# Storing token rows and their norm factors together, after the first score rows, in a fused attention and expert kernel

## The chip, the cores and the metric

The kernel runs on one core of a Trainium2 chip. The metric is device time in microseconds of one execution; lower is better. The engines are TensorE (PE, matrix products and transposes), VectorE (DVE), ScalarE (ACT), GpSimd (POOL) and SyncE (SP, which only issues DMAs here). Each takes its instructions in program order. The core's DMAs run on sixteen DMA engines. A DMA with run-time row numbers (a gather or a scatter) is issued by POOL.

## The reference

`x` is 8 x 256 tokens of 256 values in float32, 2048 tokens in all. Four blocks follow, each added to `x`:

```python
x = x + L0_xattn(layernorm(x), ctx, ctx)    # correlation attention
x = x + L0_ffn(layernorm(x))                # eight experts, balanced
x = x + L1_xattn(layernorm(x), ctx)         # 16-head softmax attention
x = x + L1_ffn(layernorm(x))                # shared and top-2 experts
```

The change lies in the second block. Its experts pick tokens one after another: each takes the 256 tokens with the highest score among those that no earlier expert took.

```python
def balanced_assignment(scores):
    for e in range(E):                       # E = 8, C = 256
        s = jnp.where(taken, -jnp.inf, scores[:, e])
        _, idx = jax.lax.top_k(s, C)
        parts.append(idx)
        taken = taken.at[idx].set(True)
...
routed = feat[sort_by_expert].reshape(E, C, D)
h = layer_norm(routed, ln_g, ln_b)
h = gelu(einsum("ecd,edf->ecf", h, w1) + b1)
h = einsum("ecf,efd->ecd", h, w2) + b2
out = routed + h                             # rows go back to their tokens
```

## The kernel before

`fast_path` writes out the order of all work by hand; the program order of each engine is the order of the lines. It has these stages: the correlation attention (to about 44 us); the rows that come out of it, with their norms and the expert scores (44 to 55); seven searches for the experts' thresholds, with the expert products beside them (55 to about 222); the softmax attention; the last experts.

**Rows and factors.** `X` holds the tokens in SBUF, 128 partitions by 16 tiles of 256 values. `copy_rows` puts the rows of a batch into PSUM with a product by the identity, `spread_rows` adds the attention's output, and `take` (line 2006 issues its store) or `act_sums` (line 2023) copies the sum back to `X`, takes its statistics, and stores the rows of that batch on SP into `NMd`, a DRAM table of 2048 rows of 258 floats. The last two floats of a row are its norm's scale and shift (`rm`); `store_factors` (line 1944) writes these with four DMAs of 512 pieces of 8 bytes.

**Scores.** `SC` holds the scores, and SP stores it to DRAM (`SCd`, line 2178). `load_row(e)` (line 2170) reads expert e's row of it back, spread over all partitions: four groups of tokens, 32 copies of each. After the score store SP issues, in this order: rows 1 and 2, the four factor stores, rows 3 to 6, a 2 MB store of zeros to `Yd` (the experts' output table, line 2183), and one of zeros to the spare rows of `Od` (line 2187).

**Searches.** `search(e)` finds expert e's threshold in five rounds. In each round DVE counts the scores above 32 trial levels (`above`, line 2203), PE sums the counts over partitions (`pcn`, line 2220), and DVE picks the next level (`few`, line 2225, `t`, line 2230). `list_tokens(e)` then turns the choice into 256 row numbers (`pid` on PE, `ids` on DVE) and lets POOL gather those rows and their factors from `NMd` into `R` (line 2341), with two DMAs of 128 rows.

**The work beside them.** `work` is a queue of small PE pieces. `fill(us)` takes pieces from its front until their planned cost has used up `us`:

```python
while work and us > 0.3:
    cost, do = work.popleft()
    do()
    us -= cost
```

The queue starts with 32 steps of `keys` and 20 of `vals` (planned at 0.43 each, one product of 256 columns per step, two steps to a tile). The second step of a tile ends with an ACT copy (`KT` or `VA`) that frees its PSUM slot in `ps_k`, which has two. `search` calls `fill(head)` before its first round's sum, `fill(each[r - 1] - 0.86)` before each later one, and `fill(0.86)` after each of the first four. `FILLS` gives `head` and `each`. Steps of `steps_of(e)` run after each of these rounds.

`ffn(e, ...)`, called by `start_ffn`, normalises the two gathered tiles on ACT (line 2383), puts `turn_rows` (four transposes and two ACT operations that give `RT`) at place 3 of `work`, and appends 16 `up` steps (`ph`) and 16 `down` steps (`py`), then the load of expert e+2's weights (`load_l0`). Before the change the first expert's `ffn` is called after search 1 ends; expert e's, for later ones, in the third round of search e+2.

Of the kernel before, what the change touches and what calls it, by code (L numbers as in the profile page):

```python
# [9 lines left out]
F32 = mybir.dt.float32  # L10
# [9 lines left out]
P = 128  # L20
# [1066 lines left out]
def fast_path(  # L1087
# [33 lines left out]
    nc = tc.nc  # L1121
# [26 lines left out]
    res = ctx.enter_context(tc.tile_pool(name="res", bufs=1))  # L1148
    small = ctx.enter_context(tc.tile_pool(name="small", bufs=3))
    dram = ctx.enter_context(tc.tile_pool(name="dram", bufs=1, space=DRAM))  # L1150
    X = res.tile([P, NT, D], F32, name="X")
    hn = ctx.enter_context(tc.tile_pool(name="hn", bufs=2))
    nfine = res.tile([P, 1], F32, name="nfine")
    bad0 = res.tile([P, 1], F32, name="bad0")
# [684 lines left out]
    def copy_rows(b, pool, tag):  # L1839
        pos[b] = pool.tile([P, TPB, D], F32, tag=tag, name="po")  # L1840
        nc.tensor.matmul(  # L1841
            pos[b].rearrange("p h d -> p (h d)"),
            ident,
            rows_of(b).rearrange("p h d -> p (h d)"),
            start=True,
            stop=False,
            skip_group_check=True,
        )
# [90 lines left out]
    rowv = NMd.rearrange("(c p) d -> p c d", p=P)  # L1939
    sexp = pa.tile([P, NT, 32], F32, name="sexp")  # L1940

    def store_factors(m):
        for h in range(TPB):
            nc.sync.dma_start(
                out=NMd.rearrange("(g m h p) d -> m h p g d", m=2, h=TPB, p=P)[m, h][
                    :, :, D:
                ],
                in_=rm[:, 8 * m : 8 * m + 8, :].rearrange(
                    "p (g h) d -> h p g d", h=TPB
                )[h],  # L1950
            )


    psrs = []
# [41 lines left out]
    def take(bs, raw=False):  # L1996

        for b in bs:
            for h in range(TPB):
                q = TPB * order_b.index(b) + h  # L2000
                if raw:
                    nc.vector.bn_stats(st6[:, q, :], pos[b][:, h, :])
                else:
                    tile_stats(MV[:, q, :], pos[b][:, h, :])
            nc.scalar.copy(rows_of(b), pos[b])
            nc.sync.dma_start(
                out=rowv[:, TPB * b : TPB * (b + 1), 0:D], in_=rows_of(b)
            )

    sums = pa.tile([P, NT, 2], F32, name="sums")  # L2010
    sq = pa.tile([P, D], F32, name="sq")
# [1 line left out]
    def act_sums(b):  # L2013

        for h in range(TPB):
            q = TPB * order_b.index(b) + h
            nc.scalar.activation(
                rows_of(b)[:, h, :],
                pos[b][:, h, :],
                AF.Identity,  # L2020
                accum_out=sums[:, q, 0:1],
            )
        nc.sync.dma_start(out=rowv[:, TPB * b : TPB * (b + 1), 0:D], in_=rows_of(b))
        qs = slice(TPB * order_b.index(b), TPB * order_b.index(b) + TPB)
        nmean = small.tile([P, TPB], F32, tag="nmean", name="nmean")
        nc.gpsimd.tensor_scalar(nmean, sums[:, qs, 0], -1.0 / D, None, ALU.mult)
        nc.gpsimd.tensor_scalar(MV[:, qs, 0], sums[:, qs, 0], 1.0 / D, None, ALU.mult)

        def squares():
            for h in range(TPB):  # L2030
                q = TPB * order_b.index(b) + h
                nc.scalar.activation(
                    sq,
                    rows_of(b)[:, h, :],
                    AF.Square,
                    bias=nmean[:, h : h + 1],
                    accum_out=sums[:, q, 1:2],
                )
            nc.gpsimd.tensor_scalar(
                MV[:, qs, 1], sums[:, qs, 1], 1.0 / D, None, ALU.mult  # L2040
            )

        return squares
# [84 lines left out]
    raw_means()  # L2128
    means_a()
    means_2()  # L2130
    means_3(nc.gpsimd)

# [42 lines left out]

    nc.sync.dma_start(out=SCd, in_=SC)
    rows = {e: load_row(e) for e in range(1, 3)}
    for m in range(2):  # L2180
        store_factors(m)
    rows.update({e: load_row(e) for e in range(3, E - 1)})
    nc.sync.dma_start(
        out=Yd.rearrange("(c p) d -> p c d", p=P),
        in_=blank[:, 0:D].unsqueeze(1).to_broadcast([P, NT, D]),
    )
    nc.sync.dma_start(out=Od[T:, :], in_=blank[:, 0:D])

    def search(e, row, steps, head, each):

# [185 lines left out]
    def ffn(e, ids, R):  # L2376

        w1, w2, b2b = W0.pop(e)
        RT = pf.tile([P, KC, CAP], F32, tag="RT", name="RT")
        A = pf.tile([P, NF, CAP], F32, tag="A", name="A")  # L2380
        Y = pf.tile([P, NCT, D], F32, tag="Y", name="Y")
        for r in range(NCT):
            nc.scalar.activation(
                R[:, r, 0:D],
                R[:, r, 0:D],
                AF.Identity,
                bias=R[:, r, D + 1 :],
                scale=R[:, r, D : D + 1],
            )
            if e in TPART and r == NCT - 1:  # L2390

                nc.scalar.copy(blank[:, D : D + 1], blank[:, D + 1 : D + 2])
                n0_, n1_ = TPART[e]
                nc.sync.dma_start(
                    out=Td.rearrange("(n p) w -> p n w", p=P)[:, n0_:n1_, :],
                    in_=blank.unsqueeze(1).to_broadcast([P, n1_ - n0_, ROW]),
                )

        def turn_rows():
            prt = ps_t.tile([P, KC, NCT, P], F32, tag="pt", name="prt")  # L2400
            for r in range(NCT):
                for kc in range(KC):
                    nc.tensor.transpose(
                        prt[:, kc, r, :], R[:, r, kc * P : (kc + 1) * P], ident
                    )
            for kc in range(KC):
                nc.scalar.activation(  # L2407
                    RT[:, kc, :],
                    prt[:, kc].rearrange("p r q -> p (r q)"),
                    AF.Identity,  # L2410
                    bias=gbc[:, 1, kc : kc + 1],
                    scale=gbc[:, 0, kc : kc + 1],
                )

        work.insert(min(3, len(work)), (0.5, turn_rows))

        def up(f):
            ph = ps_h.tile([P, CAP], F32, tag="ph", name="ph")
            for kc in range(KC):
                nc.tensor.matmul(  # L2420
                    ph,
                    w1[:, kc, f * P : (f + 1) * P],
                    RT[:, kc, :],
                    start=(kc == 0),
                    stop=(kc == KC - 1),
                )
                if kc < KC - 1:
                    yield
            nc.scalar.activation(  # L2429
                A[:, f, :], ph, AF.Gelu_apprx_tanh, bias=b1c[:, e, f : f + 1]  # L2430
            )
            yield

        def down(r):
            py = ps_k.tile([P, D], F32, tag="pm", name="py")
            for f in range(NF):
                nc.tensor.matmul(  # L2437
                    py,
                    A[:, f, r * P : (r + 1) * P],
                    w2[:, f, :],  # L2440
                    start=(f == 0),
                    stop=(f == NF - 1),
                )
                if f < NF - 1:
                    yield
            if e < 3:
                nc.scalar.copy(Y[:, r, :], py)
                nc.gpsimd.tensor_tensor(Y[:, r, :], Y[:, r, :], b2b, ALU.add)
            else:
                nc.vector.tensor_tensor(Y[:, r, :], py, b2b, ALU.add)  # L2450
            nc.gpsimd.indirect_dma_start(
                out=Yd,
                out_offset=bass.IndirectOffsetOnAxis(ap=ids[:, r : r + 1], axis=0),
                in_=Y[:, r, :],
                in_offset=None,
            )
            yield

        if e == E - 1:
            work.append((0.0, lambda: first_rows(False)))  # L2460
        for f in range(NF):
            in_steps(up(f), KC)
        if e == E - 1:
            final.append(Y)
            work.append((0.0, lambda: first_rows(True)))
        for r in range(NCT):
            in_steps(down(r), NF)
        if e + 2 < E:
            work.append((0.0, lambda: W0.update({e + 2: load_l0(e + 2)})))
# [17 lines left out]
    def steps_of(e):  # L2487

        for r in range(ROUNDS - 1):
            if e >= 2:  # L2490
                next(listers[e - 1], None)
            if 2 <= e < 6:
                move_x(4 * (e - 2) + r)
            if r == 2 and e >= 2:
                start_ffn()
            yield

    FILLS = {0: (1.29, [1.29] * 4), 1: (2.15, [1.29] * 4)}
    FILLS[2] = FILLS[3] = (2.15, [1.73, 2.58, 1.73, 1.73])
    for e in range(E - 1):  # L2500
        if e == 5:
# [14 lines left out]
        if e == 0:  # L2516
            for k, _ in enumerate(listers[0]):
                fill((0.86, 0.43, 1.29, 0.43)[k])
        elif e == 1:
            start_ffn()  # L2520
    last = [listers[E - 2], list_tokens(E - 1, hand_over)]
    for k in range(5):
        for lister in last:
# [982 lines left out]
```

## Time and profile before

| what | us |
|---|---|
| median of 6 runs | 883.55 (881.74 to 885.25) |
| the profiled execution, its own time | 884.3 |
| its span, first to last instruction | 882.6 |
| PE busy | 860.2 (97%) |
| DVE / ACT / POOL busy | 307.9 / 268.3 / 219.1 |
| mean granted TensorE clock | 0.992 |

Times inside the execution are counted from the first instruction. A busy PE means that it had a product under way; at a granted clock of 0.50 the same product takes twice as long. In a timeline a row gives start, duration, engine, line, operation, output and inputs, and in brackets the engine's idle time just before it and what is named as ending it. Where an instruction waited for several things, the one that came last by the profile is named, and if that had long been done, it was another. SP's rows are the issuing of DMAs, not the transfers.

### The profile page before, as it was taken

Reading aid. Unit: us, or ns where it says so; the run is one execution under the profiler, and the core shown is the slowest. Engines: PE = TensorE matmul, PEld = TensorE weight load, DVE = VectorE, ACT = ScalarE, POOL = GpSimd, SP = SyncE. Lnnn points to the kernel's source line nnn. Section 1 sums busy time; section 2 is a strip of 40 time slices with the busy share of each in tenths; the row PEclk is TensorE's granted clock in tenths of the full one; section 3 lists DMA queues with packets and bytes.
Section 4 is the critical chain, followed back from the end, with each engine's and each line's share of the span. In section 5 each row is a group of like instructions: output and inputs, shape, how many; then the busy total and the mean of one; then the engine's idle time right before and its main releaser. Section 6 shows DMA issues by size and latency. Waiting matters only on the chain.

```text
span 882.6 us, 11174 instructions
## 1 busy us (share of the span) xinstructions
PE 860.2 (97%) x4192; PEld 535.7 (61%) x4192; DVE 307.9 (35%) x1008; ACT 268.3 (30%) x500; POOL 219.1 (25%) x305
## 2 busy tenths in 40 slices
PE   8998899999999999999999999999999999999997
PEld 6655687778555555545658474746464656474746
DVE  7475777430646765552111212111111111111011
ACT  4353454242577766331010111121111111111110
POOL 7161232321326464323310020111111122111200
PEclk9998899999999999999999999999999999999999
DMA  8475357950330001271110636565646433311130
GB/s 248 161 221 171 130 151 223 320 192 30 113 98 25 2 14 38 52 290 49 68 56 25 191 110 178 155 179 153 181 149 174 159 93 109 89 13 12 15 105 28
DMA packets 87126, 105.22 MB, mean 119 GB/s; under 512 B 8824, under 2 KB 77656, under 8 KB 87032
## 3 DMA queue, kind: packets, MB, share of 16 engines
q1 hardware_dynamic: 78520, 91.10, 32.4%
q0 software_dynamic: 7920, 13.02, 6.9%
q8 instruction: 35, 0.57, 0.3%
q10 hardware_dynamic: 624, 0.30, 0.1%
q14 instruction: 27, 0.22, 0.1%
HBM read 80.60 MB, written 25.37 MB: 120 GB/s over the span
## 4 chain that ended last, share of the span: by engine, by line
PE 90%; DMA 4%; DVE 3%; POOL 2%; ACT 1%; issue 1%; SPq 0%; DVEq 0%; POOLq 0%
PE pgt L3126 19%; PE py L3148 19%; PE pu L3126 19%; PE py L2437 6%; PE ph L2420 6%; PE p L2703 4%; PE pv L2718 3%; DMA R<-NMd,ids 2%; PE pp L2769 2%; PE pp L2670 2%; PE pp L1392 1%; PE pp L1413 1%; PE po L1841 1%; PE pgu L3321 1%; DMA C<-in_ctx_dram 1%; PE pt L3182 1%
## 5 line engine op out<-in xcount | busy, mean ns | idle before, releaser
L3135 DVE TENSOR_TENSOR A<-A,pu 128x512 f32<-128x512 f32 x96 | 66.1, 688 | 365.1 <-PE pu L3126 358.4
L3134 ACT ACTIVATE A<-pgt 128x512 f32<-128x512 f32 x96 | 57.4, 598 | 271.4 <-PE pgt L3126 271.4
L3195 POOL DMA_INDIRECT Od<-Y,ids x32 | 49.5, 1548 | 305.2 <-ACT Y L3208 208.6
L3126 PE MATMUL pgt<-RT,wa 128*128 128x512 f32 x256 | 121.1, 595 | 0.0
L3126 PE MATMUL pu<-RT,wb 128*128 128x512 f32 x256 | 120.3, 592 | 0.0
L3148 PE MATMUL py<-wc,A 128*128 128x256 f32 x512 | 111.8, 379 | 0.0
L3148 PEld LDWEIGHTS py<-wc,A 128*128 128x128 f32 x512 | 96.7, 190 | 13.3 <-issue 0.5
L3126 PEld LDWEIGHTS pu<-RT,wb 128*128 128x128 f32 x256 | 48.6, 190 | 61.2 <-issue 60.0
L2711 ACT ACTIVATE ex<-p,scale 128x512 f32<-128x512 f32 x128 | 77.3, 690 | 27.5 <-PE p L2703 26.3
L3126 PEld LDWEIGHTS pgt<-RT,wa 128*128 128x128 f32 x256 | 47.6, 190 | 54.9 <-issue 54.5
L2420 PE MATMUL ph<-RT,w 128*128 128x256 f32 x256 | 66.7, 411 | 1.8 <-ACT RT L2407 1.6
L2437 PE MATMUL py<-w,A 128*128 128x256 f32 x256 | 61.9, 389 | 0.0
L2420 PEld LDWEIGHTS ph<-RT,w 128*128 128x128 f32 x256 | 48.1, 202 | 11.5 <-ACT RT L2407 2.3
L2437 PEld LDWEIGHTS py<-w,A 128*128 128x128 f32 x256 | 46.5, 190 | 6.5
L2943 POOL DMA_INDIRECT Td<-HP,to x32 | 31.6, 986 | 63.3 <-DMA Td<-HP,to 62.6
L2429 ACT ACTIVATE A<-ph,b1c 128x256 f32<-128x256 f32 x64 | 30.1, 473 | 55.3 <-PE ph L2420 52.2
L3126 PE MATMUL pgt<-HT,wa_-1_2749 128*128 128x512 f32 x96 | 45.5, 596 | 0.0
L3126 PE MATMUL pu<-HT,wb_-1_2750 128*128 128x512 f32 x96 | 45.1, 592 | 0.0
L3208 ACT ACTIVATE Y<-py,R 128x256 f32<-128x256 f32 x32 | 15.2, 474 | 96.5 <-PE py L3148 96.5
L2703 PE MATMUL p<-QM,KT 32*128 32x512 f32 x256 | 43.5, 640 | 0.4 <-DVE QM L2684 0.4
L3148 PE MATMUL py<-wc_-1_2751,A 128*128 128x256 f32 x192 | 41.9, 379 | 0.0
L3148 PEld LDWEIGHTS py<-wc_-1_2751,A 128*128 128x128 f32 x192 | 36.4, 190 | 5.8 <-issue 1.0
(463 smaller groups left out, 991.9 us busy)
## 6 DMA issues: line engine op xcount, KB each, us to landing
w<-in_L_ffn_w_dram SPq DMA_DIRECT2D x16, 1024.0 KB
wa<-in_L_ffn_w_e_dram SPq DMA_DIRECT2D x8, 1024.0 KB
wb<-in_L_ffn_w_e_dram SPq DMA_DIRECT2D x8, 1024.0 KB
wc<-in_L_ffn_w_e_dram SPq DMA_DIRECT2D x8, 1024.0 KB
R<-Td SPq DMA_DIRECT2D x8, 530.0 KB
sa<-in_L_ffn_w_e_dram SPq DMA_DIRECT2D x16, 256.0 KB
sb<-in_L_ffn_w_e_dram SPq DMA_DIRECT2D x16, 256.0 KB
sc<-in_L_ffn_w_e_dram SPq DMA_DIRECT2D x16, 256.0 KB
```

The costliest lines, as they stand in the source:

```text
L2420: nc.tensor.matmul(ph, w1[:, kc, f * P : (f + 1) * P], RT[:, kc, :], start=(kc == 0), stop=(kc == KC - 1),)
L2429: nc.scalar.activation(A[:, f, :], ph, AF.Gelu_apprx_tanh, bias=b1c[:, e, f : f + 1])
L2437: nc.tensor.matmul(py, A[:, f, r * P : (r + 1) * P], w2[:, f, :], start=(f == 0), stop=(f == NF - 1),)
L2703: nc.tensor.matmul(ps[g].rearrange("p m q -> p (m q)"), KT[rows, c, k0 : k0 + P], QM[b][rows, c].rearrange("p m q -> p (m q)"), start=True ...
L2711: nc.scalar.activation(e4[:, g], ps[g], AF.Exp, scale=scale)
L2718: nc.tensor.matmul(pvs[b, c][32 * g : 32 * g + 32, m, :], VA[:, b * TPB + kt, 8 * c + 2 * g + m, :], ex[b, c, kt][:, g, m, :], start=(kt = ...
L2943: nc.gpsimd.indirect_dma_start(out=Td, out_offset=bass.IndirectOffsetOnAxis(ap=to[g][:, k, j : j + 1], axis=0), in_=HP[:, GT * g + j, :], ...
L3126: nc.tensor.matmul(ps, w_[:, kc, fs], xs[kc], start=(kc == 0), stop=(kc == KC - 1),)
L3134: nc.scalar.activation(a, pgt, AF.Silu)
L3135: nc.vector.tensor_tensor(a, a, pu, ALU.mult)
L3148: nc.tensor.matmul(py, A[:, f, s : s + P], wc[:, f, :], start=(f == 0), stop=(f == NF - 1))
L3195: nc.gpsimd.indirect_dma_start(out=Od, out_offset=bass.IndirectOffsetOnAxis(ap=ids, axis=0), in_=Y, in_offset=None, compute_op=ALU.add,)
```

## The change

Six edits in `fast_path`:

1. `X` becomes a view of a wider tile `XF` with 258 floats per row, so that a row and its two factors lie side by side. Rows of two tiles are no longer adjacent, and `copy_rows` passes them as three-dimensional operands.
2. `keep_factors(m)` copies the factors from `rm` into `XF` on POOL; it is called before and after the last `means_3`. `store_factors` goes.
3. The stores of rows in `take` and `act_sums` go. Four stores of four tiles each, rows and factors together, stand on SP behind the loads of score rows 1 and 2.
4. The load of row 3, the zeros to `Yd` and `Od` and the loads of rows 4 to 6 move to the first expert's `ffn`, behind its two normalisations. A copy of one element of `blank` on ACT, which stands behind them, holds the zero stores back.
5. The first expert's `ffn` is called in the third round of search 1, not after search 1. Its `turn_rows` goes to place 6 of the queue.
6. `FILLS[0]` takes one step fewer in two rounds of search 0.

```diff
-    X = res.tile([P, NT, D], F32, name="X")
+    XF = res.tile([P, NT, D + 2], F32, name="X")
+    X = XF[:, :, 0:D]
...
-            pos[b].rearrange("p h d -> p (h d)"),
+            pos[b],
             ident,
-            rows_of(b).rearrange("p h d -> p (h d)"),
+            rows_of(b),
...
-    def store_factors(m):
-        for h in range(TPB):
-            nc.sync.dma_start(
-                out=NMd.rearrange("(g m h p) d -> m h p g d", m=2, h=TPB, p=P)[m, h][
-                    :, :, D:
-                ],
-                in_=rm[:, 8 * m : 8 * m + 8, :].rearrange(
-                    "p (g h) d -> h p g d", h=TPB
-                )[h],
-            )
+    def keep_factors(m):
+        nc.gpsimd.tensor_copy(
+            XF[:, :, D:].rearrange("p (g m h) d -> p m g h d", m=2, h=TPB)[:, m],
+            rm[:, 8 * m : 8 * m + 8, :].rearrange("p (g h) d -> p g h d", h=TPB),
+        )
...
             nc.scalar.copy(rows_of(b), pos[b])
-            nc.sync.dma_start(
-                out=rowv[:, TPB * b : TPB * (b + 1), 0:D], in_=rows_of(b)
-            )
...
-        nc.sync.dma_start(out=rowv[:, TPB * b : TPB * (b + 1), 0:D], in_=rows_of(b))
...
     means_2()
+    keep_factors(0)
     means_3(nc.gpsimd)
+    keep_factors(1)
...
     nc.sync.dma_start(out=SCd, in_=SC)
     rows = {e: load_row(e) for e in range(1, 3)}
-    for m in range(2):
-        store_factors(m)
-    rows.update({e: load_row(e) for e in range(3, E - 1)})
-    nc.sync.dma_start(
-        out=Yd.rearrange("(c p) d -> p c d", p=P),
-        in_=blank[:, 0:D].unsqueeze(1).to_broadcast([P, NT, D]),
-    )
-    nc.sync.dma_start(out=Od[T:, :], in_=blank[:, 0:D])
+    for i in range(0, NT, 4):
+        nc.sync.dma_start(out=rowv[:, i : i + 4, :], in_=XF[:, i : i + 4, :])
...
+            if e == 0 and r == NCT - 1:
+                nc.scalar.copy(blank[:, 0:1], blank[:, 1:2])
+                rows.update({n: load_row(n) for n in range(3, 4)})
+                nc.sync.dma_start(
+                    out=Yd.rearrange("(c p) d -> p c d", p=P),
+                    in_=blank[:, 0:D].unsqueeze(1).to_broadcast([P, NT, D]),
+                )
+                nc.sync.dma_start(out=Od[T:, :], in_=blank[:, 0:D])
+                rows.update({n: load_row(n) for n in range(4, E - 1)})
...
-        work.insert(min(3, len(work)), (0.5, turn_rows))
+        work.insert(min(3 if e else 6, len(work)), (0.5, turn_rows))
...
-            if r == 2 and e >= 2:
+            if r == 2:
                 start_ffn()
...
-    FILLS = {0: (1.29, [1.29] * 4), 1: (2.15, [1.29] * 4)}
+    FILLS = {0: (1.29, [1.29, 0.86, 1.29, 0.86]), 1: (2.15, [1.29] * 4)}
...
-        elif e == 1:
-            start_ffn()
```

## The prediction

> **What bounds the kernel now.** I read the page's chain by engine first, then the chain in order of time, then the timelines around the only long pause it shows.
>
> ```profile
> PE 90%; DMA 4%; DVE 3%; POOL 2%; ACT 1%; issue 1%; SPq 0%; DVEq 0%; POOLq 0%
> 73.94 6.55 DMA R<-NMd,ids
> ```
>
> TensorE (PE) sets the end, so time is won only where PE pauses or runs slowly. The largest DMA piece near the change is the first expert's gather. Its surroundings, from the timelines of SP, POOL, ACT and PE (start us, us, engine, line):
>
> ```profile
> 33.24 0.36 SPq L1786 DMA_DIRECT2D Wd<-wrow  x1
> 35.38 0.36 SPq L1792 DMA_DIRECT2D CW<-Wd  x1
> ...
> 55.81 0.33 SPq L2178 DMA_DIRECT2D SCd<-SC  x1
> 60.91 1.26 SPq L2170 DMA_DIRECT2D row<-SCd  x2
> 62.28 4.65 SPq L1944 DMA_DIRECT2D NMd<-rm  x4
> ...
> 71.38 2.72 SPq L2183 DMA_DIRECT2D Yd<-blank  x1
> ...
> 72.39 1.25 POOL L2341 DMA_INDIRECT R<-NMd,ids  x1 [8.67 <-PE pp L1413]
> 73.94 0.97 POOL L2341 DMA_INDIRECT R<-NMd,ids  x1 [0.30 <-issue]
> ...
> 80.51 0.60 ACT L2383 ACTIVATE R<-R 128x256 f32<-128x256 f32 x1 [1.09 <-DMA R<-NMd,ids]
> ...
> 82.51 1.22 PE L2420 MATMUL ph<-RT,w 128*128 128x256 f32 x2 [0.66 <-ACT RT L2407]
> 83.53 0.23 PE L2220 MATMUL pcn<-B32h,cnt 128*128 128x32 f16 x1
> ...
> 102.94 0.55 PE L2322 MATMUL pid<-ob,oab 128*16 128x16 f16 x16 [1.52 <-DVE ob L2318]
> 105.05 0.80 PE L2420 MATMUL ph<-RT,w 128*128 128x256 f32 x1 [0.96 <-ACT RT L2407]
> ```
>
> The indices were ready at 67.9 (cast `ids`, 67.71 for 0.17), but the gather began at 72.39: the releaser named is not the cause. In the trace's DMA completions, the last of the four factor stores completes at 71.31. The second gather then lands behind the 2 MB of zeros at 80.49. PE stands almost idle from 77.40 to 82.51. The clock column of the windows shows the sequel (us, then sum and count by engine, clock, DMA share, GB/s; the last two rows are PE alone):
>
> ```profile
> 54.00:58.00 4.00, 3.97 (x21) 2.56 (x17) 3.50 (x16) 2.09 (x5) 2.44 (x10) 1.00 1.08 270
> 76.00:80.00 4.00, 1.84 (x9) 1.10 (x8) 2.40 (x8) 0.60 (x1) 0.00 (x0) 1.00 1.07 384
> 82.00:84.00 2.00, 1.49 (x4) 1.12 (x5) 0.20 (x2) 0.92 (x2) 0.00 (x0) 0.50 0.26 97
> ...
> 76.76:80.18 3.42, 1.08 (x5) 1.00 1.07 383
> 100.66:104.07 3.41, 1.89 (x25) 1.00 0.43 115
> ```
>
> PE was busy for 32% of the first 3.4 us stretch, 55% of the second; after each the clock was 0.50 for 6.83 us (80.18 to 87.00, 104.07 to 110.90, from the trace's clock record). The second hole comes because the queue of PE work runs dry in the fourth search.
>
> **The change part by part.**
>
> *Score row earlier.* The eight row stores (2 MB, 44 to 59) no longer stand ahead of the score store. That store took 5.10 us (55.81 to the row issue at 60.91); the 256 KB store at 33.24, with nothing ahead, 2.14. So the row loads issue near 57.95 instead of 60.91.
>
> *Stores of rows with factors.* `keep_factors` adds two POOL copies, about 0.25 us each by the neighbouring small POOL operations (0.20 to 0.25), ending near 58.6, before SP gets there; POOL's later work is covered by its 8.67 us wait. Rows 1 and 2 count four DMA completions each, stores sixteen: the loads run on four engines, 97 GB/s at a share of 0.26 (row 82 to 84), so 2.7 us each. First packets come 1.55 us after issue as before, so they occupy these four until 59.5+5.4 = 64.9. The new stores, 2.1 MB or 132 KB an engine, queue behind. At 384 GB/s in all (the zeros) that is 5.5 us, at 270 (the old row stores) 7.8; I take 7.0, nearer the latter because the row pitch of 1032 bytes is the same. Data ends at 71.9; completion 0.5 to 1.3 later, 0.7 taken; the gather began 1.1 after the last completion before (0.3 after its indices for the second expert). So the first gather starts near 73.4, an estimate: no earlier than before. What improves is its flight: no zeros beside it. The second starts 1.5 later, lands in 3.3 (the first gather's twelve undisturbed engines) to 3.8 (the shortest in the trace): 78.4 instead of 80.49. Bounds: 75.8 with every lower price (gathers 1.25 apart), 81.5 with rows at their old 6.5 us and every higher one.
>
> *First expert's work in the second search.* I counted the deferred queue from the code: 52 steps of 0.46 us, ten gone before the searches. Search 0 takes 13 instead of 15, its lister 7, so 22 are left at search 1 instead of 20; after its third round nine. There the normalisation enters ACT. Before the next count (`pcn`, round 4) PE must do the first matmul of a value tile whose PSUM slot (two in the pool) is freed by an ACT copy queued *behind* the two normalisations. Thus the added wait stops ACT, then PE, then the search: PE runs out at 75.35 (the round from 74.29 less one step), and goes on at landing + 0.6 (norm) + 0.25 (blank copy) + 0.37 (VA copy) = 79.6. Round 4's count runs at 80.1 instead of 75.82. Then two steps, the transposes and two steps (2.55 us at full clock) lead to the first count of search 2. The idle stretch, about 4 us, is still long enough for half clock from 80.2: they take about 4.3, so that count is at 84.4 against 83.53, **0.9 later**. But PE is now fully busy from 80.2, where before it was 1.77 of 3.41; I expect full clock at 83.6 instead of 87.0, half of 3.4: **1.7 gained**. (If it lasts to 87.0 as before: 0.5 lost instead of 0.8 gained.)
>
> *Two steps more left.* They go to the dry spot in search 3: the 1.52 us pause shrinks to 0.6, paying back the two steps, and the stretch at 55% rises to about 80%. Stretches with 2.71 and 2.15 of 3.41 busy (162.10 and 179.16) kept full clock. So the second half-clock spell should vanish: 5.85 us of work (105.05 to 110.90) at half pace, **2.9 gained**.
>
> *At nothing.* Search 0 keeps its 1.53 us rounds, since count 0.84, few 0.27, t 0.22 and pcn 0.19 fill them without the steps. Row 3 lands near 84, needed at 95.53; zeros land near 90, first scatter into them at 98.77; rows 4 to 6 until some 98, needed at 110.89. [...] Expert 1's gather (95.04) meets rows 5 and 6; even the 6.55 of the disturbed gather leaves it in time for 102.21. The strided X: the same counts of PE, ACT and DVE operations, inner runs still 256 elements; if its eight row products (0.59) and eight copies (0.59) lost a tenth, 0.9 us.
>
> Sum: +0.9 -1.7 -2.9 = -3.7. The profiled execution took 884.3 (span 882.6, 1.7 around it), so 880.6; the median is 0.75 lower than that execution, so 879.9.
>
> [...]
>
> **Rivals.**
>
> 1. *Bigger gain.* The stores land early (gather landing by 77): the hole is under 2.7 us, splits over two stretches, and no half clock follows. At 76.8, count at 81.1 (-2.4), 1.7 of slow clock, 2.9 of the second: -7.0, 876.5. For it: issue on SP is free from 59. Against: four engines hold rows first.
> 2. *Second spell stays.* The remaining pauses, 0.6 and 0.96, fall within one 3.4 us stretch (PE busy 54% of it, like the 55% before). Then -0.8: 882.8. The change would seem to do nothing.
> 3. *Slower: ACT's queue head.* The gather lands at 81.5; the copy frees PSUM at 82.7, and five steps and the transposes at half clock bring search 2's count to 87.9, 4.4 late; 1.7 back; with the second spell kept +2.7, 886.2. It decides from a landing of about 80.6. Against: even then an avoided second spell cancels it.
> 4. That the early start does not bind (gather landing before 74.5) I exclude by the four engines' 12 us of queue from 59.5.
>
> **How the numbers follow.** Forecast (-2 to -5) 0.40, rival 1 0.23, rival 2 (within 1.8) 0.20, rival 3 0.17. About 0.2%, 1.8 us, is what a measurement here can tell from no change. So faster 0.63, same 0.20, slower 0.17. Low end 876.0, just beyond rival 1; high end 885.3, the edge of "same", leaving out most of rival 3 and the tail below.
>
> **What would show it.** Right: row loads issued near 58; the first gather still after 72; its second landing 77 to 80; round 4's `pcn` in search 1 after 78 with PE idle before it and ACT waiting for the gather; one half-clock spell of 3.4 us near 80, none near 104. Wrong: a gather before 71 (the stores do not queue behind the rows), two spells of 6.8 us as before, or a new pause at expert 1's gather or at row 3.

## The result, and the profile after

The changed kernel took 883.25 us (median; 880.75 to 884.91) against 883.8 us for the kernel before (879.58 to 885.79) in the same rounds: ratio 0.9992, interval [0.9986, 0.9999]. On a second chip (experiment b1) it took 883.47 against 882.92, ratio 1.0014 [1.0004, 1.0024]. Both lie within 0.2% and on either side of one: no change that can be told. The profiled execution took 885.06 us (span 883.3, granted clock 0.993). The forecast was 879.9.

The chain by engine, and its first pieces by line, of the changed kernel:

```profile
PE 89%; DMA 4%; DVE 2%; POOL 2%; ACT 1%; issue 1%; SPq 0%; POOLq 0%; DVEq 0%
PE pgt L3123 19%; PE py L3145 19%; PE pu L3123 19%; PE py L2436 6%; PE ph L2419 5%; PE p L2700 4%; PE pv L2715 3%; DMA R<-NMd,ids 2%; PE pp L2766 2%; PE pp L2667 2%; PE pp L1415 1%; DMA NMd<-X 1%; PE po L1843 1%; PE pgu L3318 1%; DMA C<-in_ctx_dram 1%; PE pt L3179 1%
```

The shares by engine are nearly those of before. New on the chain is `DMA NMd<-X`: the stores of rows and factors now stand ahead of the first gather. The timelines of SP, POOL, ACT and PE of the changed kernel:

```profile
56.12 0.34 SPq L2173 DMA_DIRECT2D SCd<-SC  x1
58.29 1.26 SPq L2165 DMA_DIRECT2D row<-SCd  x2
59.66 4.72 SPq L2176 DMA_DIRECT2D NMd<-X  x4
64.42 2.92 SPq L2165 DMA_DIRECT2D row<-SCd  x1
...
75.15 1.25 POOL L2330 DMA_INDIRECT R<-NMd,ids  x1 [10.59 <-DVE few L2214]
...
78.41 0.60 ACT L2372 ACTIVATE R<-R 128x256 f32<-128x256 f32 x1 [4.25 <-DMA R<-NMd,ids]
79.46 0.60 ACT L2372 ACTIVATE R<-R 128x256 f32<-128x256 f32 x1 [0.45 <-DMA R<-NMd,ids]
79.97 0.17 ACT L2381 COPY blank<-blank 128x1 f32<-128x1 f32 x1
80.05 0.64 ACT L1424 COPY VA<-pp 128x256 f32<-128x256 f32 x2
...
80.47 1.22 PE L1415 MATMUL pp<-wkv_in,CT 128*128 128x256 f32 x2 [4.76 <-ACT VA L1424]
81.48 0.23 PE L2209 MATMUL pcn<-B32h,cnt 128*128 128x32 f16 x1
85.96 0.23 PE L2209 MATMUL pcn<-B32h,cnt 128*128 128x32 f16 x1
```

Read from below. PE stood for 4.76 us until an ACT copy freed a slot in PSUM. That copy stood on ACT behind the blank copy and two normalisations, and these waited for the gather. POOL issued the gather at 75.15, 1.1 after the last completion of the stores (74.07 in the trace's DMA records); the DVE operation named in its row is not what it waited for, since in a1 and b2 below the gather moves with the stores (to 71.57 and 72.02). On twelve of the sixteen DMA engines the last store was complete at 67.69 already; the other four took until 74.07. Search 1's last count (81.48) was 5.66 us later than before, and search 2's first one (85.96) 2.43 later. The clock, by windows of the changed kernel (us, PE's busy time and count, clock, DMA share, GB/s):

```profile
76.20:79.61 3.41, 0.00 (x0) 1.00 0.28 78
79.61:83.03 3.42, 2.56 (x7) 0.50 0.57 193
83.03:86.44 3.41, 3.41 (x12) 0.50 1.03 347
103.51:106.92 3.41, 2.02 (x24) 1.00 0.75 201
106.92:110.33 3.41, 3.41 (x11) 0.50 0.57 191
```

In this stage two spells at half clock remain: 79.61 to 86.44 (6.83 us, as long as before) and 106.92 to 110.33 (3.41, half as long as before). By search 2's second count the loss has shrunk from 2.43 to 1.03 us (88.32 against 87.29), because the kernel before ran at half clock until 87.00, well past its first count; by search 4's first count it is 0.11 (113.32 against 113.21).

### The profile page after: what moved, and what is told of

The parts are those of the page before. It is cut to its first block, busy times and chain, and to the rows that moved or that the text cites. A ratio compares the mean times of both kernels' runs of the same rounds, so it can differ in the third digit from the quotient of the medians.

```text
span 883.3 us, 11158 instructions
## 1 busy us (share of the span) xinstructions
PE 859.2 (97%) x4192; PEld 535.4 (61%) x4192; DVE 307.7 (35%) x1008; ACT 268.2 (30%) x501; POOL 218.2 (25%) x307
## 4 chain that ended last, share of the span: by engine, by line
PE 89%; DMA 4%; DVE 2%; POOL 2%; ACT 1%; issue 1%; SPq 0%; POOLq 0%; DVEq 0%
PE pgt L3123 19%; PE py L3145 19%; PE pu L3123 19%; PE py L2436 6%; PE ph L2419 5%; PE p L2700 4%; PE pv L2715 3%; DMA R<-NMd,ids 2%; PE pp L2766 2%; PE pp L2667 2%; PE pp L1415 1%; DMA NMd<-X 1%; PE po L1843 1%; PE pgu L3318 1%; DMA C<-in_ctx_dram 1%; PE pt L3179 1%
## 5 line engine op out<-in xcount | busy, mean ns | idle before, releaser
L2419 PE MATMUL ph<-RT,w 128*128 128x256 f32 x256 | 63.5, 396 | 0.8 <-ACT RT L2406 0.7
```

Of the source, the lines that this page charges most:

```text
L2419: nc.tensor.matmul(ph, w1[:, kc, f * P : (f + 1) * P], RT[:, kc, :], start=(kc == 0), stop=(kc == KC - 1),)
```

## The experiments

**Theory.** The gather waits for the stores, the stores wait on the four DMA engines that are still busy with the score rows, and the normalisations that wait for the gather close ACT to the copies that PE needs. The pause of PE (4.76 us) is then charged again by the clock (6.83 us at half clock). **Rivals:** that the zeros, which ran beside the gather before, set its landing; and that the rearranged stores themselves are worth nothing. In the tables below, differences are against the kernel before on the same chip.

**a1: only row 1 ahead of the stores.**

```diff
-    rows = {e: load_row(e) for e in range(1, 3)}
+    rows = {1: load_row(1)}
     for i in range(0, NT, 4):
         nc.sync.dma_start(out=rowv[:, i : i + 4, :], in_=XF[:, i : i + 4, :])
+    rows[2] = load_row(2)
```

> The changed kernel with score row 2 loaded behind the four stores instead of ahead of them. Queue theory (the stores wait on the four engines that load score rows, and the gather waits for the stores): last store completion about 2.7 us earlier, 71.4 instead of 74.07, first gather near 72.5 instead of 75.15, second gather landing near 76.8 instead of 79.44, PE's pause in search 1 about 2 us instead of 4.8, time 2.7 to 5 us under the changed kernel (about 878.5 to 880.5). Rival (the stores are late for another reason, their number of pieces or SP's issuing): gather stays within 1 us of 75.15 and the time does not move.

882.1 us, 0.9986 [0.9971, 1.0001]; 878.5 to 880.5 had been expected. Timelines of POOL, ACT and PE of a1:

```profile
71.57 1.25 POOL L2331 DMA_INDIRECT R<-NMd,ids  x1 [7.15 <-PE pcn L2210]
...
77.84 1.09 ACT L2373 ACTIVATE R<-R 128x256 f32<-128x256 f32 x2 [3.83 <-DMA R<-NMd,ids]
...
79.33 1.22 PE L1415 MATMUL pp<-wkv_in,CT 128*128 128x256 f32 x2 [3.77 <-ACT VA L1424]
```

One row less ahead of the stores lets the gather start 3.6 us sooner: the stores do queue behind the rows. But it landed only 1.5 us sooner. The trace's completions say why: the first gather was done on twelve engines by 74.81, and on the four that carried rows 2 and 3 only from 76.44 to 77.61. The rows behind the stores thus delay the gather on those four engines, though POOL issues it and SP the rows.

**a2: the early start undone** (edits 5 and 6 of the change).

```diff
-        work.insert(min(3 if e else 6, len(work)), (0.5, turn_rows))
+        work.insert(min(3, len(work)), (0.5, turn_rows))
...
-            if r == 2:
+            if r == 2 and e >= 2:
...
-    FILLS = {0: (1.29, [1.29, 0.86, 1.29, 0.86]), 1: (2.15, [1.29] * 4)}
+    FILLS = {0: (1.29, [1.29] * 4), 1: (2.15, [1.29] * 4)}
...
+        elif e == 1:
+            start_ffn()
```

> The changed kernel with the first expert's work called after search 1 again (place 3, the old FILLS). Queue-head theory (the normalisations ahead of the VA copies on ACT stop PE before round 4): round 4's count of search 1 back near 76.1 instead of 81.5, gather unchanged near 75.15 and 79.4, search 2's first count near 82.8 instead of 86.0; two steps fewer are left for search 3, so its pause is back to 1.5 us. Time 0 to 2 us under before. If the early start is what earns the changed kernel's small gain: 1 to 3 us over the changed kernel.

881.3 us, 0.9976 [0.9963, 0.999]. The gather began at 74.73 and landed at 79.03, much as in the changed kernel, but round 4's count came at 75.77, and PE waited for the rows only where it needs them. PE's timeline of a2:

```profile
78.70 0.44 PE L2402 MATMUL prt<-ident,R 128*128 128x128 f32 x2 [1.35 <-ACT R L2372]
```

Search 2's first count came at 81.33, 4.63 sooner than in the changed kernel. The rest of the change thus gains about 0.24% by itself (interval 0.1 to 0.37%); the early start, with the gather landing where it does, takes most or all of that back in search 1. The pause in search 3 returned with it (1.52 us, as before).

**a3: the kernel before, with only the zero stores held back** behind the first expert's normalisations (the blank copy and the two stores moved; nothing else).

> The kernel before with only the two stores of zeros held back behind the first expert's normalisations. If the zeros slowed the gather's flight: gathers issued at 72.4 and 73.9 as before, second landing near 77.3 instead of 80.49, search 2's first count near 80.5 instead of 83.5, time about 3 us under before (half-clock spells kept) to 5 (first one gone). If the flight is slow for another reason: landing at 80.5, time as before.

883.6 us, 1.0005 [0.9989, 1.0022]. ACT's timeline of a3:

```profile
80.19 0.60 ACT L2377 ACTIVATE R<-R 128x256 f32<-128x256 f32 x1 [0.65 <-DMA R<-NMd,ids]
```

The second gather landed at 80.16 (before: 80.49), so the zeros alone did not set it. On twelve engines it was there at 77.0; on the four it came from 79.92 to 80.16, behind rows 3 and 4 (completions 75.08 and 78.16). In the kernel before, all sixteen completions lie between 79.84 and 80.49. The zeros had thus held the twelve engines as long as the rows held the four, and taking away one of the two left the landing where it was. The prediction, which put it down to the zeros alone, had half of the cause.

**a4: eight products to fill the pause.** Their result is not used.

```diff
+            if e == 1 and r == ROUNDS - 1:
+                pfill = ps_h.tile([P, CAP], F32, tag="ph", name="pfill")
+                for _ in range(8):
+                    nc.tensor.matmul(
+                        pfill, ident, XF[:, 0, 0:CAP], start=True, stop=True
+                    )
             fill(each[r - 1] - 0.86 if r else head)
```

> The changed kernel with eight products of 256 columns whose result nobody reads, put on PE ahead of round 4's step in search 1, in the idle stretch from 75.7 to 80.5; they take about 3.7 us at full clock. Clock theory (the pause costs a half-clock spell of 3.4 to 6.8 us on top): no half clock near 80, time 1.7 to 3.4 us under the changed kernel. If the clock is not what costs: the same time as the changed kernel, or up to 0.5 us more.

880.74 us, 0.9976 [0.9961, 0.9991]. PE's timeline of a4, then its windows:

```profile
80.20 0.70 PE L1415 MATMUL pp<-wkv_in,CT 128*128 128x256 f32 x2 [1.15 <-ACT VA L1424]
```

```profile
80.00:84.00 4.00, 3.80 (x20) 1.00 0.81 271
100.50:103.92 3.42, 2.16 (x24) 1.00 0.75 229
```

Work that is of no use gained time: the value product came at 80.20 instead of 80.47, hardly sooner, but at full clock, and search 2's first count came at 83.05 instead of 85.96. The spell near 80 was gone; the one near 104 came all the same, after a stretch in which PE was busy 2.16 of 3.42 us.

**b1: the changed kernel again, on the second chip.**

> The changed kernel itself, beside the experiments on one chip. All theories: 0.5 to 1 us under the kernel before; the runs spread over 3 to 4 us with the number of half-clock stretches, which differs from run to run.

883.47 us, 1.0014. PE's pause was 4.95 us, the gather began at 75.23: the same picture.

**b2: rows 1 to 3 loaded over all sixteen engines.** Each is read as four DMAs of 32 partitions, so that no access has an outer dimension of four.

```diff
-        nc.sync.dma_start(
-            out=row,
-            in_=bass.AP(
-                sd.tensor, sd.offset + e * TB, [[32 * TB, 4], [0, 32], [1, TB]]
-            ),
-        )
+        for g in range(4 if e <= 3 else 0):
+            nc.sync.dma_start(
+                out=row[32 * g : 32 * g + 32, :],
+                in_=bass.AP(
+                    sd.tensor, sd.offset + (32 * g + e) * TB, [[0, 32], [1, TB]]
+                ),
+            )
...
```

Rows 4 to 6 keep the old load.

> The changed kernel with score rows 1 to 3 each loaded by four DMAs of 32 partitions, whose outer dimension of 32 spreads each over sixteen engines instead of one DMA on four. Queue theory: no engine holds rows ahead of the stores; stores complete by 68 to 71 instead of 74.07 (SP issues eight row DMAs first, some 4 us), first gather near 70 to 72, second landing 74 to 75.5, so the normalisations no longer stop PE before round 4 (pause under 1 us instead of 4.76), no half clock near 80, time 5 to 7 us under the changed kernel. Rival (the four engines are not what delays the stores): gather within 1 us of 75.15.

878.6 us, 0.9955 [0.994, 0.997]. Timelines of SP, POOL and PE of b2:

```profile
57.98 3.59 SPq L2166 DMA_DIRECT2D row<-SCd  x8
61.66 3.41 SPq L2184 DMA_DIRECT2D NMd<-X  x4
...
72.02 1.25 POOL L2338 DMA_INDIRECT R<-NMd,ids  x1 [7.76 <-DVE t L2227]
...
77.36 1.22 PE L1415 MATMUL pp<-wkv_in,CT 128*128 128x256 f32 x2 [1.92 <-ACT VA L1424]
```

Each of the eight row DMAs now counts sixteen completions, where a row of the changed kernel counts four, and the last of them came at 63.22 (67.14 in the changed kernel); all stores were complete at 71.25 instead of 74.07, though SP spent 2.3 us more on issuing rows. The pause shrank from 4.76 to 1.92 us, not below 1 as expected, and the half clock to one stretch (77.39 to 80.80). The gather of a1 shows that a transfer from another queue comes late on those engines too (77.61 against 74.81); with rows 1 to 3 spread, all sixteen completions of that gather lie between 74.74 and 75.07.

**b3: the value copies of the last tiles on DVE instead of ACT**, so that the waiting normalisations are ahead of no copy.

```diff
-        in_steps(vals(i, 1, ps_k), KC)
+        in_steps(
+            vals(i, 1, ps_k, nc.vector.tensor_copy if i >= 11 else nc.scalar.copy), KC
+        )
```

> The changed kernel with the PSUM copies of the last five value tiles on VectorE instead of ScalarE, so that none stands behind the normalisations. Queue-head theory: round 4's count of search 1 near 76.5 instead of 81.5, PE's pause moves to the transposes (77.5 to 80.5) and shrinks from 4.8 to about 3 us, search 2's first count near 82.5 instead of 86.0, time 2.5 to 3.5 us under the changed kernel. If the queue head is not the cause: no change, or 0.5 us more for the copies on VectorE.

878.89 us, 0.9959 [0.9944, 0.9975]. The gather began at 75.22 and landed at 79.56, as late as in the changed kernel. PE's timeline of b3:

```profile
76.44 0.19 PE L2211 MATMUL pcn<-B32h,cnt 128*128 128x32 f16 x1 [0.23 <-DVE above L2194]
...
79.13 0.44 PE L2404 MATMUL prt<-ident,R 128*128 128x128 f32 x2 [1.53 <-ACT R L2374]
80.24 0.44 PE L2404 MATMUL prt<-ident,R 128*128 128x128 f32 x2 [0.68 <-ACT R L2374]
```

Round 4's count came at 76.44 instead of 81.48. The pause of 4.76 became two of 1.53 and 0.68, and the clock stayed full in the whole stretch (1.00 from 76.00 to 82.83). So the head of ACT's queue, not the landing as such, was the long pause.

**b4: b2 and a2 together** (rows spread, the early start undone).

> Rows 1 to 3 spread as in the kernel above, and the first expert's work called after search 1 as before the change (place 3, the old FILLS). Queue theory: landing near 75 means that the rows are there when search 2's three steps and the transposes come (77.4), so PE's pause is only the wait for the normalised rows on ACT (about 1 us), no half clock near 80, search 2's first count near 79.5; the pause of 1.5 us in search 3 stays. Time 4 to 6 us under before. If an early start is worth more than this: the kernel with the early start and spread rows is 1 us or more faster.

877.59 us, 0.9945 [0.9931, 0.9959]. The second gather landed at 76.06 and PE did not wait before the transposes. The pause in search 3 (1.52 us) and its half clock (99.06 to 105.89) were back.

**c1: b2 and b3 together.**

> The changed kernel with both cures: score rows 1 to 3 spread over sixteen engines, and the copies of the last five value tiles on VectorE. Both causes lie on one path (late rows, then ScalarE's queue head), so the gains do not add: second landing near 76.3 as with spread rows, round 4 of search 1 near 76.4, no pause over 1 us before the transposes, search 2's first count near 79.5 to 80. Time 1 to 2 us under either cure alone (about 877), no half clock near 80. If the causes were separate: 8 us under the changed kernel (875).

877.67 us, 0.9934 [0.9922, 0.9946]: the fastest kernel by ratio, but not faster than b4 by more than the intervals allow. PE's timeline of c1:

```profile
77.08 0.60 PE L2412 MATMUL prt<-ident,R 128*128 128x128 f32 x4
...
79.29 0.70 PE L1415 MATMUL pp<-wkv_in,CT 128*128 128x256 f32 x2 [1.17 <-DVE VA L1424]
```

The transposes no longer wait, and one new pause of 1.17 us stands behind DVE. The gains of b2 and b3 (4.3 and 4.0 us) do not add up to 8: they remove the same pause.

**c2 and c3: the kernel before, with b2's row loads, and c3 with the zeros held back as well.**

> The kernel before with nothing but score rows 1 to 3 spread over sixteen engines. Queue theory: the factor stores are no longer behind the rows, last completion near 68 instead of 71.31, first gather near 69 instead of 72.4; the zeros still come after it and hit the second gather, landing 74 to 77 instead of 80.49; search 2's first count 78 to 80 instead of 83.5. Time 3 to 5 us under before. If the whole rearrangement of stores was needed for an early gather: within 1 us of before.

> The kernel above with the zero stores held back behind the first expert's normalisations too. Queue theory: first gather near 69, both landed by 74, so the rows are there before search 1 ends; search 2's first count near 79; time equal to or up to 1 us under the kernel above, and within 1 us of the changed kernel with the late start and spread rows. If storing rows and factors together is worth something by itself: 2 us or more over that one.

c2: 879.68 us, 0.9955 [0.9941, 0.9968]; c3: 879.01 us, 0.9947 [0.9926, 0.9969]. POOL's timeline of c2:

```profile
70.40 1.25 POOL L2349 DMA_INDIRECT R<-NMd,ids  x1 [6.66 <-DVE t L2238]
```

Spreading three row loads brings the kernel before to where it brings the changed one (0.9955 both). The rows landed later than expected (in c2 the second gather at 78.99, against 74 to 77; in c3 at 77.55, against 74); rows 4 to 6 keep the old load there, which counts four completions a row in the kernel before (row 4 at 77.70 to 78.35), but no run shows that they are the reason. And c3 is level with b4 (0.9945), which differs from it in storing rows and factors at once and in loading rows 4 to 6 behind the zeros: with the rows spread, that part of the change is worth nothing that can be told. The intervals of c2 and c3 overlap, so what holding the zeros is worth there stays open.

All kernels together. "Gap" is the time from search 1's second count to search 2's first, from PE's timelines; it holds the pause, its half clock and the same products but for a step or two:

| kernel | second landing | gap | median less that of before |
|---|---|---|---|
| before | 80.49 | 12.31 | 0 |
| changed | 79.44 | 14.46 | -0.55 |
| b1, changed again | 79.62 | 14.19 | +0.55 |
| a1 | 77.94 | 13.46 | -0.9 |
| a4 | 79.18 | 11.66 | -2.3 |
| b2 | 76.33 | 10.62 | -4.3 |
| b3 | 79.56 | 9.81 | -4.0 |
| c1 | 76.15 | 8.60 | -5.6 |
| a2, late start | 79.03 | 10.20 | -1.7 |
| a3, late start | 80.16 | 11.63 | +0.6 |
| b4, late start | 76.06 | 7.80 | -5.3 |
| c2, late start | 78.99 | 10.53 | -3.6 |
| c3, late start | 77.55 | 8.72 | -4.2 |

Among kernels with the same start the time mostly follows the gap, not the landing (b3 lands as late as the changed kernel). The seven rows of kernels with the early start are faster by 1.3 to 2.7 us more than their gaps say, the five with the late one by -1.3 to 1.8. The ranges overlap; their means differ by 1.7, so an estimate is that the early start gains 1.5 to 2 us later on. In search 1 it costs more than that unless ACT or the gather is freed (a2's gap is 4.3 us shorter than the changed kernel's). Gaps are of one profiled execution each, so a single row is good to about a microsecond.

## Why the prediction was wrong, step by step

The sum had three terms: 0.9 lost to search 2's first count, 1.7 gained because half clock would end at 83.6, and 2.9 gained because the second spell would not come. They came as 2.1 lost (2.43, less the 0.32 by which this execution runs late), 1.4 gained and 0.9 gained. The steps that lead to the late gather and to ACT's queue head held as mechanisms; the two that were to bring the gain, the end of half clock and the missing second spell, failed.

*Row loads earlier: right.* Issued at 58.29, forecast 57.95; this profiled execution runs 0.32 late from about 33 us on, while the second round's counts of search 0 in the later kernels scatter from 57.40 to 57.86, with the strided `X` and without it, so no cost of the strided `X` can be told from it.

*Stores behind the rows on four engines: right, but mis-sized by 1.2 us.* From row 2's last completion (67.14) the stores took 6.9 us, forecast 7.0; from their end to the gather 1.1, as in the kernel before (the forecast's 73.4 leaves 0.8 for it, 0.3 short of its own figure). The wrong term is the rows: 1.55 and twice 2.7 us from a transfer rate, 64.9. The first row took 5.94 us from issue to completion, the second 2.9 more. In a1, where row 1 stood alone, it took 6.3, and the trace of before has the same in its completions: issued at 60.91, complete at 66.94 and 69.78. Those 8.87 us, added to 57.95, give 66.8, and with the late start 67.14. The time needed was there, and the prediction used it for its upper bound alone (the old 6.5 us); its sum took a rate.

*The gather's flight: 0.6 us shorter than the lowest price, and half right in cause.* The second landing came at 79.44 (forecast 78.4), 2.75 us after its issue (forecast 3.3 to 3.8). a3 shows that the zeros had not been the only delay before: the rows on the four engines held it as long. Row 3 did not land near 84 either: the blank copy holds only the zero stores, SP issued row 3 right behind the stores at 64.42, and it landed at 76.68.

*ACT's queue head: right.* PE ran out at 75.71 (forecast 75.35) and went on 1.03 us after the landing (forecast 1.2); b3 took the copies out of ACT's queue, and round 4's count came 5.0 us sooner with the same landing. The first count of search 2 was to be 0.9 us later and was 2.4: of the 1.5 between, 0.3 is the late start, 0.5 the rest of PE's later return (80.47 against 79.6), 0.7 more time at half clock.

*Release of the half clock at 83.6: failed.* It held until 86.44. PE went on at 80.47, not 79.6, so the stretch from 79.61 held 2.56 us of work in 3.42, and the clock stayed at half. By search 2's second count the changed kernel was to be 0.8 us ahead, and was 1.03 behind. In b2 PE went on at 77.36, 0.03 us before its stretch began, and half clock ended after that one stretch. The prediction's own parenthesis, half clock to 87.0, is the branch that came, with the later landing on top.

*The second spell: mostly failed, 2.0 of 2.9 us.* PE's timeline of the changed kernel there:

```profile
103.83 0.55 PE L2311 MATMUL pid<-ob,oab 128*16 128x16 f16 x16 [0.52 <-DVE ob L2307]
104.75 0.93 PE L2402 MATMUL prt<-ident,R 128*128 128x128 f32 x4 [0.37 <-ACT R L2372]
106.33 0.70 PE L2419 MATMUL ph<-RT,w 128*128 128x256 f32 x2 [0.65 <-ACT RT L2406]
```

The pauses shrank as forecast, to 0.52, 0.37 and 0.65 us, but all three fell into one stretch, as rival 2 had it for two: it was 59% busy (2.02 of 3.41), not 80%, and half clock followed. That 59% had to bring it is not shown: in a3 a stretch at the same place in search 3, busy 1.90 of 3.42 (98.74 to 102.16, five stretches after the start of that run's half-clock one at 81.68), kept the full clock. The spell lasted one stretch instead of two. From search 3's first count to search 4's (98.16 to 113.32) the changed kernel took 15.16 us, the kernel before 16.08 (97.13 to 113.21): 0.9 gained.

So the outcome is rival 2's, no change: a loss of 2.1 us to search 2's first count (2.4 less the late start), 1.4 of it given back by that search's second count, since the kernel before was still at half clock there, and 0.9 in search 3: 0.2 us ahead, less than can be told. What stays open is why the same kernel's executions differ by 4 to 7 us (877.94 to 885.05 for the kernel before on the chip of a1 to a4): its 34 spans there rise by 0.48 us for each us of half clock (least squares, 0.6 us left over), so the number of half-clock spells carries most of it, but what sets the number in an execution is not shown.

## What to carry to other kernels

Do not put an instruction that waits for a DMA ahead of the copies that free PE's PSUM slots on the same engine: here that turned a late gather into a pause of PE of 4.76 us, with 6.83 us at half clock behind it, and with those copies on another engine (b3) pauses of 1.53 and 0.68 us at full clock were left. Here, loads whose outer dimension is four held up what was queued behind them on four DMA engines (stores to 74.07 against 67.69 on the other twelve in the changed kernel), another queue's gather included (77.61 against 74.81 in a1); four DMAs with 32 partitions outermost (b2, c2) were worth 0.45%, where the whole change was worth nothing that can be told. Take the time of a transfer from its completions in the trace rather than from a rate: rows 1 and 2 of the changed kernel took 8.85 us from issue to the last completion, 6.95 by the prediction's rate.

## What the runs showed of the hardware

- A gather on POOL's queue finished on twelve engines at 74.81 and on the four that carried SP's rows at 77.61 (a1; in a3, its second gather, 77.0 and 80.16).
- In the clock records of the kernel before and the changed one the spells at half clock near 80 and 105 lasted 3.41 or 6.83 us, and the two began seven (80.18, 104.07) and eight (79.61, 106.92) times 3.41 us apart; the stretches here are counted from such starts. Half clock followed stretches of 3.41 us in which PE was busy 59% (changed kernel) and 63% (a4), and ended after one busy 3.15 of 3.42 us (c1, 99.69 to 103.11) or more; 2.56 of 3.42 (changed kernel, from 79.61) was not enough. In the changed kernel's stretch (103.51 to 106.92) no pause was longer than 0.65 us. The busy share alone does not decide when it begins either: 56% (a3, 98.74 to 102.16) and 2.15 of 3.42 us (kernel before, from 179.16) kept the full clock. What decides is not shown.
- Filling a pause with products that are thrown away kept the clock full there and made the kernel about 2.3 us faster than the kernel before (a4).
